# Exponentials read back in one piece, two rows sent through DRAM, the last norm on ScalarE, and a new table of due times

## The chip, the cores and the metric

The kernel runs on one core of a Trainium2 chip. A core has a matrix engine (TensorE, PE; its weight loads are listed as PEld), a vector engine (VectorE, DVE), an engine for activation functions (ScalarE, ACT), a general engine (GpSimd, POOL) and a queue engine (SyncE, SP). Each runs its own list of instructions in order and waits on semaphores for the others. SBUF and PSUM are the on-chip memories, DRAM the memory off the core's engines; 16 DMA engines move data between SBUF and DRAM, and in this kernel SP issues all of the transfers. The metric is the device time of one execution in microseconds (us), taken as a median.

## The reference

There are 64 independent graphs of 256 nodes with 256 features, each with a dense 256 x 256 matrix `adj`. Four layers follow each other, each wrapped as `x = layernorm(x + layer(x, adj))`; all is float32.

```python
# layer 0, 4 heads
att = sigmoid(q @ k.T * scale);  adj_h = adj * att
dis = where(deg > 0, deg ** -0.5, 0)         # deg: row sums of adj_h
Y = (dis[:, None] * adj_h * dis[None, :]) @ X;  layernorm of Y
# layer 1, 8 heads
out = softmax(where(adj > 0, q @ k.T / sqrt(32), -9e15)) @ v;  out @ Wo
# layer 2
h = ((adj @ x) + eps * x) @ W1                # 256 -> 1024
h = silu(h * rsqrt(mean(h ** 2) + 1e-6) * w);  h @ W2
# layer 3
Wh = x @ W;  e = leaky_relu(s1[:, None] + s2[None, :], 0.2)   # s = Wh @ a
h = softmax(where(adj > 0, e, -9e15)) @ Wh;  gelu(layernorm(h))
```

After layer 3 comes the last residual layernorm, and its result is written out.

## The kernel before, in words

**Tiles.** A graph's 256 x 256 matrix is one SBUF tile of 128 partitions x 512: two blocks of 128 rows side by side. A PSUM tile of 128 x 512 holds one result; there are eight. A matmul with a full 128 x 128 weight block and 256 columns takes 379 ns in the profile, and a product of two 256 x 256 matrices is eight of them. Heads are packed: products over 32 or 64 rows (L610, L517) or columns (L654, L557) of the array run beside each other, and the array changes its tiling between such groups and full ones.

**Recording.** The function `graph` records the operations of one graph, and `weights` those that load the constants. An `Op` has its engine, a cost, what it reads and writes, and a due time. Nothing is emitted yet. `Plan.order` then gives every operation the time `TIMES[stage][i] + PERIOD * graph + shift`, where `SHIFTS` holds a correction for the first ten and the last ten graphs, moves it behind what it depends on, and sorts all operations of all 64 graphs by it. Each engine runs its operations in that order. So the table decides how some sixteen graphs overlap: from the sixteenth graph on, the order of every engine is one ring that repeats for each graph, with layer 3 of graph g beside layer 2 of g+3, layer 1 of g+6 and layer 0 of g+9 to g+15. While it walks through the sorted list, `Plan.order` keeps a clock for each engine from the costs, the transfers' sizes and `AFTER`, and from it takes which of the freed buffers a new value gets (`SLOTS`: 46 tiles of kind `s`, 8 PSUM tiles, and so on). The order alone is fixed; when an instruction really starts is up to the semaphores.

**Transposes through DRAM.** For most graphs a transpose is done without PE. DVE transposes blocks of 32 x 32 into `eb`, SP writes `eb` to a DRAM tile `far`, and SP reads it back in another arrangement: `far_transposed` (L341 and L345 for layer 3's `x3` and exponentials, L349 and L351 for layer 0's result) and `far_shuffled` (L365, L368) for layer 1's input. Layer 1's exponentials of four heads (1 MB) are written in one piece (L638) and read back by four DMAs of 256 KB, one for each 32 partitions (L640). The 16 reciprocals of layer 1's softmax go the same way: `rT` is written (L662), and eight DMAs spread each head's row over 32 partitions as `rb` (L664). SP must wait for a write to land before it issues the reads, and everything behind it in SP's order waits too. The first graph or two, and the last three, use PE for some transposes (`NEAR`), because there PE has room.

**1/rms in layer 2.** The squares are summed over features by DVE (L712, L714) and PE (L719), DVE transposes the sums (L724), and POOL takes the power -1/2 (L727, L728), with one value for each token on its partition. PE then transposes this column, broadcast over 128 columns, into a PSUM tile `pr` (L734): a row of all tokens' factors on every partition. DVE multiplies `hT` by it, four of its eight feature blocks at a time (L738), ACT applies SiLU to the same four (L740), and the second product (L748) starts with the first four blocks of the first 128 tokens.

**Source terms in layer 3.** The product with `W` (L766) has two more columns, s1 and s2. ACT copies it to SBUF as `v3` (L770). PE transposes the column s2 in the same way as above into a PSUM tile (L775), and ACT adds s1 and s2 and applies the leaky relu (L779). The masked softmax follows (L479 on DVE, L484 on ACT), then the transpose through DRAM, then the product with `v3` (L395, shown as `ps<-v,eT`).

**The last norm.** `normed` scales a tile by its mean and 1/std. It does so on ACT (L433, after a small DVE step L429 that makes the bias), except for the final output `o`, which DVE scales (L437), but for the last three graphs. The statistics before it are DVE (L408) and POOL (L418, L419).

Of the kernel before, what the change touches and what calls it, by code (L numbers as in the profile page):

```python
# [10 lines left out]
AF = mybir.ActivationFunctionType  # L11
# [10 lines left out]
ITSELF = {"PE": 0, "DVE": 95, "ACT": 110, "POOL": 60, "SP": 0}  # L22
# [7 lines left out]
WORDS = {"s": 516, "d": 1024, "D": 2048, "b": 2048, "c": 32, "p": 512, "h": 2048, "t": 64, "f": 64}  # L30
# [4 lines left out]
SLOTS = {"s": 46, "d": 4, "D": 3, "b": 3, "c": 48, "p": 8, "h": 8, "t": 4, "f": 8}  # L35
DRAM = "hf"

PERIOD = 43736
TIMES = {
    "layer 0": [  # L40
        -319197, -113134, -100311, -71943, -247582, -546773, -546197, -131479, -172183, -152737, -281181, -565681,
        -397076, -73203, -63226, -95801, -374920, -232479, -110173, -195319, -301144, -87568, -115747, -89221,
        -90086, -83471, -69397, -574845, -68313, -63683, -428221, -63434, -57858],
    "y0": [
        -87831, -373130, -729274, -232310, -329503, -339824, -34600, -122314],
    "norms 0": [
        -317272, -27512, -143897, -30800, -393826, -114681, -25085, -20328, -60191, -14285, -14265],
    "x1": [
        -22878, -260036, -13056, -13194, -13556, -13246],
    "heads": [  # L50
        21083, -12704, 13821, -24706, 13005, -13170, 13837, -243391, -83618, -466639, 65818, -265435, 73110, 19862,
        -107166, -118808, 21980, 10121, -275945, 21957, 26901, 32166, 11340, -329066, -182994, -323173, -75745,
        23608, -95248, -264825, 13387, -31944, -232536, 41219, 50698, 41160, 52922, 28312, -12692, -142068, -83953,
        -450779, 19466, -393926, -133764, -346231, -789118, -242927, -827390, -284889, -296678, -73296, -150845,
        -367335, -429493, 32181, -382155, -84424, 31380, -400219, -232968],
    "layer 1": [
        -292171, -332905, -463540, -325283, -585287, 54654, -66521, -251318, -276322, -295456, -30216, 56307,
        -65386, -78434, 90307, -434932, 90241, 94160, -199479, 105185, -121163, 74219],
    "layer 2": [
        66102, 101580, 177708, 111997, -117369, -27941, 133669, -117923, -217828, -152742, -387796, 14051, 133564,  # L60
        -41433, -84629, -56243, 16618, 145648, 143272, 133937, 24587, 13427, -80823, 118404, -142608, -160852,
        137148, 118595, 74825, 145580, -289804, 60052, -166924, -3431, 150662, -168456, 169799, 100755, -8045,
        -471077, -194813, 118328, 190096, 218554, -9065, -135959, 207336, 166957, 235618, 218069, 181347, 233128],
    "x3": [
        242366, 185230, -3212, -59473, -20723, -54583, -119866, 144254, 154213],
    "layer 3": [
        276836, 259792, 276501, -11693, 283684, -160488, 83664, 237473, 286462, 287575, 288330, 294217, 114279,
        319058],
    "e3": [
        225632, 186632, 248234, -95896, 188509, 303747, 315177, 308934, 314526],  # L70
    "y3": [
        333821, 231651, 225040, 337186, 347307, 141236, 74504, 323745, 319142, 172218],
    "out": [
        334941, 353102, 351242, 369427, 456102, 453662, 446905],
    "weights": [
        -333952, -983130, -30359, -945696, -210686, -73894, -223709, -154959, -259880, -310601, -338541, -184949,
        -17446, 19612, -13322, 128972, -450356, 155594, -891871, -209532, -91470, -340360, 222543, -16205, -130618,
        97522, 87637, 248749, 277347],
    "y0 by PE": [
        -120210, -72674, -129154],  # L80
    "x1 by PE": [
        40623, 22839, -152651],
    "heads by PE": [
        -95458, 77404, 47061, -40228, 43109, -4907, 56735, -22684, 19941, -35811, 65682, 81329, -109895, -10708,
        -24959, 38549, 42640, 69976, 56753, -178021, -23198, -13718, 28668, 75592, -98145, 73422, 31198, 55531,
        51235, 24844, 60763, -27793, -9752, -23467, 70477, 25989, 2382, 78742, 63564, 1293, -164472, 35182, -52610,
        -16683, 12602, 7517, 71887, -71844, 77285, 75027, 82487, 60185, -10300, 9378, -10435, 69079, -8590, -59124,
        -58302, 76358, -3250, 77148, -45408],
    "x3 by PE": [
        269122, 230913],  # L90
    "e3 by PE": [
        314157, 165939],
    "y3 at the end": [
        325747, 321623, 301166, 221044, 338410, 229419, 304128, 177370, 248843, 349261, 270321],
    "out at the end": [
        364545, 252476, 378560, 444095, 457987, 508323, 479204, 533265],
}
SHIFTS = {
    0: (49484, -2460, -1572, -677, -2727),
    1: (4489, -16790, -1941, 1285, -26679),  # L100
    2: (-452, 1099, -750, -3702, 2374),
    3: (2324, -1473, -1339, -733, -695),
    4: (-50857, -1286, 113, -692, -3911),
    5: (-742, -320, -1324, 277, 36812),
    6: (103, 289, -690, -555, 30699),
    7: (-196, 1000, 88, -352, 20200),
    8: (651, 1253, -472, -442, 34933),
# [116 lines left out]
def two(v):  # L224

    return v.t.rearrange("p (n c) -> p n c", n=2)
# [662 lines left out]
```

## Time and profile before

| what | value |
|---|---|
| median of 3 runs | 2807.56 us (2806.32 to 2807.71) |
| the profiled execution | 2815.73 us |
| its span, first to last instruction | 2813.9 us |
| PE busy | 2652.4 us, 94% |
| DVE busy | 2441.4 us, 87% |
| ACT busy | 2192.5 us, 78% |
| POOL busy | 603.8 us, 21% |
| mean granted PE clock | 0.986 |
| DMA packets of the kernel's queue | 751776, 530.93 MB, 74.5% of 16 engines |

How to read it: busy time is the time in which an engine runs an instruction; registers, branches, semaphores and the issue of DMAs don't count. A group line names the source line, the engine, the operation, `out<-in` by the program's names, the shapes and the count; after the first bar stand the group's busy time in us and the mean of one in ns, after the second the time that the engine sat idle before them, and what ended most of it. A line of waits gives who waited for whom, the total in us, how often, and the longest. SPq is SP's list of DMA issues. A name such as `eT` is used for several tiles: the exponentials of layer 1 (four reads of 256 KB) and of layer 3 (four reads of 64 KB). Matmul records of one group appear as twice the program's matmuls.

### The profile page before, as it was taken

The numbers are of one execution on the slowest core, as the hardware profiler recorded it, in microseconds if no ns is written. First come the engines' busy times: TensorE is split into PE (matmuls) and PEld (weight loads), VectorE is DVE, ScalarE is ACT, GpSimd is POOL, SyncE is SP. The second block draws the span as 40 slices with busy tenths as digits, with TensorE's granted clock in tenths as the row PEclk, the third lists the DMA queues.
The fourth block names the chain that finished last, engine by engine and source line by source line (L and its number), as shares of the span: only waits on it lengthen the run. The fifth ranks groups of instructions, "written<-read, shape, count | busy, mean of one in ns | idle before, by whom it ended". The sixth has DMA issues, their size and how long they took to land.

```text
span 2813.9 us, 54722 instructions
## 1 busy us (share of the span) xinstructions
PE 2652.4 (94%) x17252; PEld 2143.6 (76%) x17252; DVE 2441.4 (87%) x6391; ACT 2192.5 (78%) x5278; POOL 603.8 (21%) x966
## 2 busy tenths in 40 slices
PE   7999999999999999999999999999999999999986
PEld 6778778887887787777877877778778778877765
DVE  4788889998999898898988988889889889989866
ACT  2778778788887887778877878788778777887776
POOL 1111212222222221212212222122122121222222
PEclk9999999999999999999999999999999999999998
DMA  4378878877878877878878778788787787787762
GB/s 135 91 206 211 204 183 202 208 211 188 215 208 198 212 197 179 210 199 189 204 185 202 196 182 211 195 190 202 187 203 196 184 203 206 192 206 199 197 137 75
DMA packets 752066, 534.44 MB, mean 190 GB/s; under 512 B 507936, under 2 KB 606624, under 8 KB 735904
## 3 DMA queue, kind: packets, MB, share of 16 engines
q1 hardware_dynamic: 751776, 530.93, 74.5%
q8 instruction: 138, 2.26, 0.4%
q14 instruction: 152, 1.25, 0.2%
HBM read 317.86 MB, written 212.86 MB: 189 GB/s over the span
## 4 chain that ended last, share of the span: by engine, by line
PE 46%; DMA 25%; DVE 19%; SPq 5%; ACT 3%; issue 3%; DVEq 0%; POOLq 0%; ACTq 0%; POOL 0%
DMA eT<-far 14%; PE ps L700 8%; PE ps L384 8%; PE ps L748 8%; PE ps L395 8%; DVE e L479 4%; DVE eb L633 4%; DMA far<-rT 4%; SPq L664 3%; PE av L654 3%; PE ps L557 2%; PE ps L517 2%; DMA far<-eb 2%; PE ps L610 2%; PE ps L766 2%
## 5 line engine op out<-in xcount | busy, mean ns | idle before, releaser
L418 POOL TENSOR_SCALAR mv<-mv 128x2 f32<-128x2 f32 x384 | 109.5, 285 | 2085.2 <-DVE mv L414 752.0
L484 ACT ACTIVATE e<-e,r 128x256 f32<-128x256 f32 x1024 | 506.0, 496 | 18.1 <-DVE r L479 17.4
L748 PE MATMUL ps<-w,hT 128*128 128x256 f32 x2048 | 462.9, 379 | 0.0
L700 PE MATMUL ps<-aggT,w 128*128 128x256 f32 x2048 | 461.9, 379 | 0.0
L700 PEld LDWEIGHTS ps<-aggT,w 128*128 128x128 f32 x2048 | 389.1, 190 | 52.9
L748 PEld LDWEIGHTS ps<-w,hT 128*128 128x128 f32 x2048 | 387.6, 190 | 52.0
L479 DVE CUSTOM_DVE_ANT_0 e<-ps,adj 128x256 f32<-128x256 f32 x1024 | 367.0, 419 | 25.0 <-PE ps L610 16.0
L419 POOL TENSOR_TENSOR mv<-mv,mhalf 128x2 f32<-128x2 f32 x384 | 331.2, 863 | 32.1
L707 ACT ACTIVATE hT<-ps,br,r 128x256 f32<-128x256 f32 x512 | 315.4, 625 | 0.0
L433 ACT ACTIVATE x<-y,mv 128x256 f32<-128x256 f32 x384 | 204.5, 595 | 131.7 <-PE ps L395 74.5
L633 DVE STREAM_TRANSPOSE eb<-e 128x1024 f32<-128x1024 f32 x248 | 289.1, 1204 | 0.0
L705 ACT ACTIVATE sq<-ps,b 128x256 f32<-128x256 f32 x512 | 241.9, 510 | 6.2 <-PE ps L700 6.2
L408 DVE BATCH_NORM_STATS2 mv<-y 128x6 f32<-128x512 f32 x320 | 222.3, 695 | 6.6
L395 PE MATMUL ps<-v,eT 128*128 128x256 f32 x512 | 141.9, 426 | 84.6 <-DMA eT<-far 41.9
L740 ACT ACT_TABLE_LOAD x63 | 80.8, 1283 | 167.4 <-DVE hT L738 167.1
L395 PEld LDWEIGHTS ps<-v,eT 128*128 128x128 f32 x512 | 102.7, 209 | 117.8 <-issue 31.0
L484 ACT ACTIVATION_READ_ACCUMULATOR e<-e,r 128x1 f32 x1024 | 192.3, 188 | 0.0
L523 DVE TENSOR_TENSOR att<-att,adjT 128x512 f32<-128x512 f32 x256 | 166.1, 674 | 14.1 <-ACT att L521 14.1
L740 ACT ACTIVATE hT<-hT 128x1024 f32<-128x1024 f32 x128 | 130.0, 1051 | 40.3 <-DVE hT L738 38.6
L654 PE MATMUL av<-eT,v 128*32 128x256 f32 x2048 | 126.7, 388 | 31.2 <-ACT x L433 20.8
L505 DVE TENSOR_TENSOR v<-ps,b_l 128x512 f32<-128x512 f32 x64 | 44.1, 690 | 127.2 <-PE ps L610 76.9
L610 PE MATMUL ps<-kT,qT 32*128 32x256 f32 x2048 | 152.0, 409 | 1.1 <-ACT kT L596 1.1
(121 smaller groups left out, 5538.8 us busy)
## 6 DMA issues: line engine op xcount, KB each, us to landing
far<-eb SPq DMA_DIRECT2D x124, 1024.0 KB, 5.6
eT<-far SPq DMA_DIRECT2D x496, 256.0 KB, 6.6
far<-eb SPq DMA_DIRECT2D x126, 256.0 KB, 2.8
xT<-far SPq DMA_DIRECT2D x496, 64.0 KB, 2.3
far<-eb SPq DMA_DIRECT2D x488, 64.0 KB, 2.8
x0T<-in_xT SPq DMA_DIRECT2D x64, 256.0 KB, 3.1
adjT<-in_adjT SPq DMA_DIRECT2D x64, 256.0 KB, 4.9
x<-in_x SPq DMA_DIRECT2D x64, 256.0 KB, 3.2
```

The lines of the kernel that those rows point to most:

```text
L384: pe.matmul(two(ps)[:, o, :], w.t[:, k, o * P:(o + 1) * P], way(two(xT)[:, k, :]), start=(k == 0), stop=(k == DB - 1))
L395: pe.matmul(two(ps)[:, n, :], two(xT)[:, k, n * P:(n + 1) * P], w()[:, k, :], start=(k == 0), stop=(k == DB - 1))
L408: op("DVE", 612, lambda: dve.bn_stats(mv.t[:, :6], src.t.rearrange("p (n c) -> p c n", n=NB)), [mv], [src])
L419: pool.tensor_tensor(m()[:, :, 0], m()[:, :, 0], c.mhalf[:, :NB], OP.pow)
L479: op("DVE", 345, lambda n=n: dve.tensor_tensor_reduce(out=E(n), in0=two(logits)[:, n, :], in1=two(negmask)[:, n, :], scale=-scale, scalar= ...
L484: op("ACT", 491, lambda n=n: act.activation(E(n), E(n), AF.Exp, bias=L(n), scale=-1.0, accum_out=r.t[:, col(n):col(n) + 1]), [(e, part(n)) ...
L633: op("DVE", 1155, lambda e=e, eb=eb, pair=pair: dve.transpose(eb.t.rearrange("p (b t g i) -> p t g b i", b=4, t=2, i=32)[:, pair], e.t.rea ...
L654: pe.matmul(two(av)[i * HD1:(i + 1) * HD1, hq, :], two(v1)[:, m, h * HD1:(h + 1) * HD1], eTs[h // 2][1](i % 2, m), start=(m == 0), stop=(m ...
L700: pe.matmul(two(ps)[:, i, :], c.w2_1.t[:, k, (j + i) * P:(j + i + 1) * P], two(aggT)[:, k, :], start=(k == 0), stop=(k == DB - 1))
L705: op("ACT", 357, lambda ps=ps, sq=sq, i=i, j=j: act.activation(two(sq)[:, i, :], two(ps)[:, i, :], AF.Square, bias=c.b2_1.t[:, j + i:j + i ...
L707: op("ACT", 452, lambda ps=ps, i=i, j=j: act.activation(Hb(j + i)[:, 0], two(ps)[:, i, :], AF.Identity, bias=c.br2.t[:, j + i:j + i + 1], ...
L748: pe.matmul(two(ps)[:, n, :], Hb(j)[:, 0, n * P:(n + 1) * P], c.w2_2.t[:, j, :], start=(j == 0), stop=(j == HB - 1))
```

## The change

- Layer 1's exponentials are written to DRAM in four pieces of 256 KB, rearranged on the way, and read back whole by one DMA of 1 MB. There are as many DMAs as before.
- For the first 61 graphs the row of 1/rms and the row of source terms no longer come from PE. A new helper `over_partitions` takes a small tile that DVE has transposed, writes it to DRAM, and reads a row from it onto all partitions by four DMAs. That is one DVE transpose and five DMAs for each of the two rows. The row lies in SBUF (kind `w`, four tiles) with its 32-token blocks in another order, which the reading instructions undo by their access patterns. The last three graphs keep the transposes on PE.
- `hT` is multiplied and passed through SiLU by halves of the tokens (all eight feature blocks of 128 tokens), not by halves of the feature blocks, and the second product needs only the half of its own tokens.
- The final norm is scaled by ACT for all graphs.
- `PERIOD`, `TIMES` and `SHIFTS` are new throughout, with stages for the new parts. So is the order of every engine, and with it the choice of buffers. Costs and sizes by which the planner's clock runs are changed (they shape the choice of buffers), there are 43 instead of 46 tiles of kind `s`, 8 instead of 4 of kind `t`, and 12 instead of 8 small DRAM tiles.

The diff, without the numbers of the tables:

```diff
-ITSELF = {"PE": 0, "DVE": 95, "ACT": 110, "POOL": 60, "SP": 0}
+ITSELF = {"PE": 0, "DVE": 130, "ACT": 110, "POOL": 60, "SP": 0}
...
-SLOTS = {"s": 46, "d": 4, "D": 3, "b": 3, "c": 48, "p": 8, "h": 8, "t": 4, "f": 8}
+SLOTS = {"s": 43, "w": 4, "d": 4, "D": 3, "b": 3, "c": 48, "p": 8, "h": 8, "t": 8, "f": 12}
...
-PERIOD = 43736
+PERIOD = 49305
...
+    def over_partitions(src, at):
+        far, dst = Value("f", "far"), Value("w", "row", 4)
+        op("SP", 500, lambda: nc.sync.dma_start(far.t, src.t), [far], [src], after=2600, size=36)
+        for q in range(4):
+            op("SP", 500, lambda q=q: nc.sync.dma_start(
+                dst.t[32 * q:32 * q + 32].rearrange("p (a m) -> p a m", a=4),
+                far.t.rearrange("(a c) m -> c a m", a=4)[at][None].to_broadcast([32, 4, 64])), [(dst, q)], [far], after=1900, size=37)
+        return dst
...
     def normed(src, name):
-        if name != 'o' or b >= plan.graphs - ENDS:
-            op("DVE", 70, lambda: dve.scalar_tensor_tensor(
-                m()[:, :, 1], m()[:, :, 1], -1.0, m()[:, :, 0], op0=OP.mult, op1=OP.mult), [mv], [mv])
+        op("DVE", 70, lambda: dve.scalar_tensor_tensor(
+            m()[:, :, 1], m()[:, :, 1], -1.0, m()[:, :, 0], op0=OP.mult, op1=OP.mult), [mv], [mv])
...
-            op("DVE", 328, lambda n=n: dve.tensor_scalar(
-                two(dst)[:, n, :], two(src)[:, n, :], m()[:, n, 1:2], m()[:, n, 0:1],
-                op0=OP.subtract, op1=OP.mult), [(dst, n)], [(src, n), mv])
+            op("ACT", 492, lambda n=n: act.activation(
+                two(dst)[:, n, :], two(src)[:, n, :], AF.Identity, bias=m()[:, n, 1:2], scale=m()[:, n, 0:1]),
+                [(dst, n)], [(src, n), mv])
...
-            eb, far, eT = Value("D", "eb", 2), Value("h", "far"), Value("D", "eT", 4)
+            eb, far, eT = Value("D", "eb", 2), Value("h", "far", 4), Value("D", "eT")
...
-        op("SP", 500, lambda eb=eb, far=far: nc.sync.dma_start(far.t, eb.t), [far], [eb], after=5500, size=700)
         for q in range(4):
-            op("SP", 500, lambda far=far, eT=eT, q=q: nc.sync.dma_start(
-                eT.t[32 * q:32 * q + 32].rearrange("j (a g) -> j a g", a=4),
-                far.t.rearrange("(a j) (b g) -> b j a g", a=4, b=4)[q]), [(eT, q)], [far], after=5000, size=178)
+            op("SP", 500, lambda eb=eb, far=far, q=q: nc.sync.dma_start(
+                far.t.rearrange("(b j) (a g) -> a j b g", a=4, b=4)[q],
+                eb.t[32 * q:32 * q + 32].rearrange("j (b g) -> j b g", b=4)), [(far, q)], [eb], after=2000, size=180)
+        op("SP", 500, lambda far=far, eT=eT: nc.sync.dma_start(eT.t, far.t), [eT], [far], after=2400, size=850)
...
-    hT = Value("b", "hT", HB)
+    hT = Value("b", "hT", NB * HB)
...
+    last = " by PE" if b >= plan.graphs - NEAR[2] else ""
+    if last:
+        ...
+        op("PE", 2 * PE_TR, fn, [pr], [rs], mode="transpose")
+    else:
+        back, by = Value("t", "back"), "p (a n i) -> p n a i"
+        op("DVE", 163, lambda: dve.transpose(back.t, rs.t), [back], [rs])
+        pr = over_partitions(back, 0)
-    for j in range(0, HB, 4):
-        four = [(hT, i) for i in range(j, j + 4)]
-        op("DVE", 1130, lambda j=j: dve.tensor_tensor(
-            Hb(j, 4), Hb(j, 4), pr.t[:, None, :N].to_broadcast([P, 4, N]), OP.mult), four, [*four, pr])
-        op("ACT", 965, lambda j=j: act.activation(Hb(j, 4), Hb(j, 4), AF.Silu), four, four, table=SILU)
+    for n in range(NB):
+        half = [(hT, NB * j + n) for j in range(HB)]
+        mine = lambda n=n: Hb(0, HB)[:, :, n * P:(n + 1) * P]
+        op("DVE", 1130, lambda n=n, mine=mine: dve.tensor_tensor(
+            mine().rearrange("p j (a i) -> p j a i", a=4), mine().rearrange("p j (a i) -> p j a i", a=4),
+            pr.t[:, :N].rearrange(by, n=NB, a=4)[:, n][:, None].to_broadcast([P, HB, 4, 32]), OP.mult), half, [*half, pr])
+        op("ACT", 965, lambda mine=mine: act.activation(mine(), mine(), AF.Silu), half, half, table=SILU)
...
-            op("PE", 4 * PE_MM, fn, [(ps, n)], [c.w2_2] + [(hT, j) for j in js] + [(ps, n)] * half)
+            op("PE", 4 * PE_MM, fn, [(ps, n)], [c.w2_2] + [(hT, NB * j + n) for j in js] + [(ps, n)] * half)
...
+    if last:
+        ...
+        op("PE", 2 * PE_TR, fn, [s2], [v3], mode="transpose")
+    else:
+        turned, by3 = Value("t", "turned"), "p (a n i) -> p n a i"
+        op("DVE", 163, lambda: dve.transpose(turned.t.rearrange("p (n k) -> p n k", n=NB), V3()[:, :, D - 30:]), [turned], [v3])
+        s2 = over_partitions(turned, 31)
...
-        op("ACT", 360, lambda n=n: act.activation(two(e)[:, n, :], s2.t[:, :N], AF.Prelu, bias=s1(n), alpha=0.2),
+        op("ACT", 400, lambda n=n: act.activation(
+            two(e)[:, n, :].rearrange("p (n a i) -> p n a i", n=NB, a=4), s2.t[:, :N].rearrange(by3, n=NB, a=4), AF.Prelu, bias=s1(n), alpha=0.2),
```

In the new order, a graph's ring on SP holds 62 DMAs (52 before). On PE the two layer 1 score groups (L610) of a graph follow the product `ps<-v,eT` at once and three groups later; before, the first stood half a ring ahead of the second.

## The prediction

> **What bounds the kernel now.** I read the busy shares first, then the stretches, the waits of TensorE (PE), and then the waits and the timeline of the queue that they lead to.
>
> ```profile
> PE 2652.4 (94%) x17252; PEld 2143.6 (76%) x17252; DVE 2441.4 (87%) x6391; ACT 2192.5 (78%) x5278; POOL 603.8 (21%) x966
> ```
>
> PE is the busy engine; its idle 161 us are what a new order can win. The stretches (span, busy time of PE, PEld, DVE, ACT, POOL, granted clock, DMA share, GB/s) show that they are not there from the start:
>
> ```profile
> 620.00:920.00 300.00, 296.17 (x1935) 242.02 (x1934) 281.46 (x723) 247.49 (x588) 69.10 (x107) 1.00 0.80 209
> 1200.00:1500.00 300.00, 283.89 (x1852) 230.94 (x1848) 265.49 (x695) 236.56 (x571) 65.08 (x105) 1.00 0.79 196
> ```
>
> From 620 to 920 us PE is 99% busy, later 95%. The timeline of PE shows one ring of each kind, from the last matmul group of one graph (`ps<-v,eT`) on:
>
> ```profile
> 607.69 1.97 PE L395 MATMUL ps<-v,eT 128*128 128x256 f32 x8 [0.69 <-DVE low L479]
> ...
> 648.10 1.89 PE L395 MATMUL ps<-v,eT 128*128 128x256 f32 x8
> ...
> 1281.08 1.97 PE L395 MATMUL ps<-v,eT 128*128 128x256 f32 x8 [1.62 <-DMA eT<-far]
> 1282.98 1.15 PE L610 MATMUL ps<-kT,qT 32*128 32x256 f32 x16
> 1284.98 1.93 PE L654 MATMUL av<-eT,v 128*32 128x256 f32 x32 [0.86 <-ACT x L433]
> ```
>
> 648.10 - 607.69 = 40.4 us a graph is PE's own work; from about the nineteenth graph on the starts of this group lie 42.5 us apart. What comes too late is `eT`, layer 3's transposed exponentials, read back through DRAM. The waits, first PE's, then those of SP, the queue that issues every DMA (total us, times, longest):
>
> ```profile
> PE ps L395 <- DMA eT<-far: 41.9, 24, 3.0
> PE av L654 <- ACT x L433: 20.8, 25, 1.1
> ...
> SPq L664 <- DMA far<-rT: 165.4, 64, 4.1
> SPq L351 <- DMA far<-eb: 164.7, 63, 5.2
> SPq L345 <- DMA far<-eb: 112.1, 68, 3.8
> SPq L345 <- DMA eT<-far: 65.0, 100, 1.1
> ```
>
> SP issues in order and stands still for a write to DRAM before it may read it back; everything behind it is late. One such place in SP's timeline:
>
> ```profile
> 1344.42 0.39 SPq L662 DMA_DIRECT2D far<-rT  x1
> 1344.90 1.04 SPq L638 DMA_DIRECT2D far<-eb  x1
> 1348.42 3.14 SPq L664 DMA_DIRECT2D rb<-far  x6
> 1351.61 2.80 SPq L640 DMA_DIRECT2D eT<-far  x6
> 1354.51 1.20 SPq L345 DMA_DIRECT2D eT<-far  x2
> ```
>
> One DMA stands between the write of `rT` and its reads, so SP waits 2.4 us; then six reads of 256 KB go out ahead of layer 3's, which need 8.0 us to land (median). From 500 to 2500 us the trace gives, per graph of 42.5 us: 52 DMAs with 26.9 us in issue (0.52 each), 2.5 us of steps between them, 1.8 us in semaphore instructions and 11.3 us of other waiting, of which some 2.6 us is for VectorE (DVE) and the rest for transfers. SP sets the pace, with no slack of its own.
>
> **What the Trainium skill says.** "DMA: Bandwidth & Descriptors", section Anatomy of one DMA, gives a DMA a fixed cost of about 2 us, most of it the receipt of the last byte; 64 KB reads here land in 2.1 us, 16 KB of `rT` in 4.0. Its Rules for kernel authors ask that a DMA which reads what another wrote waits for the first one's semaphore: that is SP's wait above. "TensorE: Matmul & The Clock Gate", section HAM oscillation, says an idle window of about 3.4 us halves PE's clock: the trace agrees, eleven spells of 3.4 or 6.8 us at half clock lie between 390 and 2720 us, mostly beside the longest waits; 51 us in all, 25 us lost. "Perfetto Trace Analysis", section Optimizing Scalar/DVE Operations, gives DVE 60 ns access on SBUF and 125 on PSUM, ScalarE (ACT) 93 and 51; here 128x512 additions take 680 ns from SBUF, 683 from PSUM, so the trace shows no such gap for DVE.
>
> **The change part by part,** per graph, 61 of 64 graphs.
>
> PE: two pairs of transposes go.
>
> ```profile
> L734 PE MATMUL pr<-ident,rs 128*128 128x128 f32 x128 | 27.5, 297 | 0.0
> L775 PE MATMUL s<-ident,v 128*128 128x128 f32 x128 | 27.5, 296 | 1.2 <-ACT v L770 1.2
> ```
>
> 55 us of busy time, but not 55 us of gain: they stood behind row-tiled matmuls, and changing tiling costs time anyway. From the fourth last L610 matmul to the third of the full group behind it: 1.03 us with a pair between, 0.86 us without; for L517 1.23 to 1.40 against 1.06. The new order also changes tiling more often. Summed by the starts of groups in the trace: before, 15 full groups of eight at 1.726, L766 1.744, the two behind transposes 1.623 and 1.622, and rows, columns and transposes 1.081 + 1.859 + 1.877 + 1.931 + 0.466 + 0.681 + 0.165 + 0.921 + 0.464: 40.32 us. After: 14 x 1.726 + 1.744, full groups behind L610, L517 and L535 at 1.919, 1.920 and 1.818, and 1.081 + 1.872 + 1.864 + 0.165 + 0.921 + 1.931 + 0.681: 40.08 us. That is -0.24 x 61 = -15 us.
>
> DVE: the last norm leaves it (2 x 0.402), its bias step (0.153) and two small transposes (0.24 each, as L724) come: -0.2 us on some 38.3. The multiplication of `hT` stays 2 x 1.21 by the SBUF/PSUM comparison above; bounds -0.1 (the skill's PSUM price) to +1.0 us (strided halves; unshown). DVE has 1.8 us of cover below 40.1; beyond that each us costs 61. ACT: +2 x 0.595 us, on 34: hidden in its 5 us of idle; without that cover +60 us. The additions of source terms read SBUF instead of PSUM: within 0.1 us. Table loads stay 3.9 a graph by the order. POOL's work is unchanged.
>
> DMA time: a packet of 2 KB takes 155 ns where the exponentials are being read, 102 where they are not, 85 to 94 as a write; 8 KB written takes 320. Exponentials before: 2 x 8 x 0.320 + 64 x 0.155 = 15.0 us on each of 16 engines. After: 64 x 0.085 to 0.102 as writes, and 2 x 8 packets of 8 KB read, between 0.320 and 0.620 (the 2 KB price by bytes): 10.5 to 16.4. I take 0.40: 12.5. The rows add ten DMAs of 128 packets of 256 B (18 ns): 1.5 us. In sum -1 us on 33 (-3 to +3).
>
> SP: 62 DMAs instead of 52. At 0.48 us for an undisturbed issue with its step that is 29.8 us; at today's mean of 0.57, 35.3. What it saves is waiting. By the new order eleven DMAs stand between `rT`'s write and the first `rb` read (before: one), fourteen between the 1/rms rows' write and read, seven for the sources, three for `yT` (before: none), thirteen for layer 3's `xT` (before: none). Of 2.6 + 2.6 + 1.8 us a graph (165.4, 164.7 and 112.1 us over 64) about 1.5 stays. Every DMA also waits for the one eight before it (seen as L345 waiting for `eT<-far`); a whole 1 MB read, by the 1 MB write's 5.6 us, holds the eighth DMA behind it 2 to 3 us. Queued behind SP's waits are then `rb`, the sources' write, `x3`'s write and the loads. 29.8 + 1.2 (slower strided issues) + 1.5 + 3 + 2 (waits for DVE) = 37.5 us, below PE's 40.1.
>
> Chain to layer 3's `eT`: the new detour adds a transpose (0.24), a write (2.7 to 4) and a read (2.3) to it, and the PE work between L766's group and the reading group falls from some 51 to 45 us by the same group times. Summing durations along the new order I get the rows landing 9 us into the ring, where ACT has idle time until the aggregate at 13; layer 3's exponentials leave DVE at 21, their write SP at 27, the reads at 31, landing at 37, needed at 40. So 3 us of slack, and what would be late next is the sources' row. First `rb`, 1/rms and exponentials have 3 to 5 us.
>
> PE's waits: L395's idle is 84.6 us, L654's 31.2. Of the 95 us that PE idles between 400 us and the drain and the 25 us of slow clock I take two thirds: -80. With -15 for PE, -4 for an earlier first matmul (its load now stands behind five DMAs instead of eight, one of them 1 MB), nothing for the drain, whose last three graphs keep the transposes: -99. Span 2813.9 - 99 = 2715, with 1.8 around it 2717; the median lies 8 below the profiled execution (2807.56 to 2815.73): 2709, say 2710 us.
>
> **The rivals.** (a) Partial: the new ring settles at 41.5 to 42 instead of 40.5, since DVE's cover is 1.8 us, or whole reads cost 0.62: 2745 to 2795 us. For it: DVE is 94% busy in the best stretch. (b) The wait only moves: the sources' row or the whole read takes `eT`'s place and the ring stays at 42.5: 2795 less PE's 15 and some noise, 2790 to 2813. For it: the order is rigid, and a single late transfer held the ring before. (c) Slower: SP is the bound. At 0.57 an issue, 35.3 us, waits above 4.8 us a graph cost PE its floor, above 7.2 the kernel is slower than now. If the 8.7 us of transfer waits of today survive, the ring is 44 us: 1.5 x 61 = +92, 2900; with 1 us less 2840. For it: ten more DMAs on the busiest queue, and single large reads. Against it: the places named above. (d) The rewritten exponential transfers do nothing, since 2 KB packets merely move to the write side: against it the 85 to 94 ns; then (a) holds.
>
> **How the numbers follow.** A measurement of this kernel tells 0.2%, 6 us. Chances: forecast (2665 to 2745) 0.52, (a) with (d) 0.20, (b) 0.07, (c) 0.21. Of (b) about half is within 0.2%. Faster 0.75, same 0.04, slower 0.21. The forecast's low end is every wait gone, 2807 - 95 - 25 - 15 = 2672; 2660 takes in cheaper reads. 2660 to 2850 leaves out little below and the worse half of (c).
>
> **What would show it.** Right: starts of the `ps<-v,eT` group 40 to 41 us apart to the end, L395's idle under 30 us, SP waits for `rT` and `yT` under 1 us a graph, DMA share not above 0.85, `eT` whole landing in 5 to 7 us. Wrong: SP without a gap and PE waiting for `rb`, `hT` or `eT`; ACT waiting for the sources' row at the Prelu over 2 us a graph; the `hT` multiplication over 1.5 us. The prediction falls if the ring is above 42.5 us.

## The result, and the profile after

| | before | after |
|---|---|---|
| median | 2807.64 us (2806.32 to 2813.96) | 3191.78 us (3183.65 to 3197.86) |
| ratio, 95% interval | | 1.1361 (1.1326 to 1.1396) |
| span of the profiled execution | 2813.9 us | 3196.1 us |

The change made the kernel 13.6% slower; 2710 us was predicted. The busy shares and the kernel's DMA queue, from the page of the kernel after:

```profile
PE 2769.7 (87%) x17008; PEld 2194.5 (69%) x17008; DVE 2427.4 (76%) x6452; ACT 2252.4 (70%) x5397; POOL 635.4 (20%) x966
...
q1 hardware_dynamic: 839616, 550.96, 62.3%
```

Of the 382 us more, 117 are PE's busy time, the rest its idle time. The share of DMA time fell (74.5% before): the packets took 1991 us on each engine instead of 2096, in a span that is 382 us longer. So the DMA engines are not short of time; they stand still in between. The same two stretches as before (span, busy time of PE, PEld, DVE, ACT, POOL, granted clock, DMA share, GB/s), and one of 6 us:

```profile
620.00:920.00 300.00, 264.42 (x1622) 210.13 (x1619) 235.10 (x618) 211.87 (x519) 61.38 (x92) 0.95 0.65 177
1200.00:1500.00 300.00, 262.01 (x1622) 208.82 (x1620) 233.75 (x621) 218.49 (x530) 60.84 (x92) 0.94 0.66 180
...
1609.00:1615.00 6.00, 3.43 (x16) 2.65 (x14) 0.00 (x0) 0.00 (x0) 0.00 (x0) 0.97 0.08 22
```

No good stretch is left, and in the third the DMA engines are 8% busy, at 22 GB/s, while DVE and ACT do nothing. SP's timeline (start, length, what is issued) shows what was in the queue then (L390 is the read of a row):

```profile
1607.45 1.88 SPq L390 DMA_DIRECT2D row<-far  x4
1609.38 0.43 SPq L352 DMA_DIRECT2D far<-eb  x1
1609.91 0.38 SPq L326 DMA_DIRECT2D adj<-in_adjS  x1
1610.33 0.45 SPq L658 DMA_DIRECT2D eT<-far  x1
1610.87 0.52 SPq L356 DMA_DIRECT2D eT<-far  x1
1611.49 2.15 SPq L680 DMA_DIRECT2D rb<-far  x1
```

The four reads of the 1/rms row land 3.9, 4.9, 6.7 and 7.6 us after their issue, the last at 1616.6. Transfers of 256 KB and of 1 MB stand in the queue behind them, and yet from 1608.5 to 1614.5 only some 71 packets of 256 B start per us. DVE waits 9.3 us for the row, and PE's matmuls behind DVE (`deg`) are late in turn; the timelines of DVE, and of PE one graph earlier:

```profile
1616.67 1.23 DVE L763 TENSOR_TENSOR hT<-hT,row 128x1024 f32<-128x1024 f32 x1 [9.34 <-DMA row<-far]
...
1524.42 1.89 PE L417 MATMUL ps<-v,eT 128*128 128x256 f32 x8
1568.96 3.78 PE L406 MATMUL ps<-xT,w_q 128*128 128x256 f32 x8 [6.85 <-DVE deg L555]
1574.82 1.89 PE L417 MATMUL ps<-v,eT 128*128 128x256 f32 x8
```

The `ps<-v,eT` groups lie 50.4 us apart here, 48.8 on average from 500 to 2500 us. The eight matmuls behind the gap take 3.78 us instead of 1.89: half clock. The Trainium skill ("TensorE: Matmul & The Clock Gate", HAM oscillation) says that an idle window of about 3.4 us halves it. In this trace each of the 51 gaps of PE that are longer is followed by half clock, but so are 14 of the 34 gaps of 1 to 3.4 us. The span holds 67 spells of half clock with 457 us in all, against 16 with 79 us before. The waits (total, times, longest):

```profile
DVE hT L763 <- DMA row<-far: 467.1, 60, 10.9
PE ps L406 <- DVE deg L555: 172.3, 33, 7.7
...
ACT e L811 <- DMA row<-far: 113.8, 23, 10.7
...
SPq L362 <- DMA far<-eb: 191.7, 49, 6.9
SPq L680 <- DMA eT<-far: 89.4, 58, 3.0
```

SP's wait for `rT` is all but gone, as forecast (7.4 us in all, 165.4 before). That for layer 0's transpose (L362) is not: its write stands behind the reads of the source terms' row and lands after 6.3 us (median from 500 to 2500 us) instead of 3.0.

### The profile page after: what moved, and what is told of

The parts are those of the page before. It is cut to its first block, busy times and chain, and to the rows that moved or that the text cites. A ratio compares the mean times of both kernels' runs of the same rounds, so it can differ in the third digit from the quotient of the medians.

```text
span 3196.1 us, 55053 instructions
## 1 busy us (share of the span) xinstructions
PE 2769.7 (87%) x17008; PEld 2194.5 (69%) x17008; DVE 2427.4 (76%) x6452; ACT 2252.4 (70%) x5397; POOL 635.4 (20%) x966
## 3 DMA queue, kind: packets, MB, share of 16 engines
q1 hardware_dynamic: 839616, 550.96, 62.3%
## 5 line engine op out<-in xcount | busy, mean ns | idle before, releaser
L440 POOL TENSOR_SCALAR mv<-mv 128x2 f32<-128x2 f32 x384 | 133.1, 347 | 1919.5 <-DVE mv L430 1448.9
L763 DVE TENSOR_TENSOR hT<-hT,row 128x1024 f32<-128x1024 f32 x122 | 148.8, 1219 | 478.5 <-DMA row<-far 467.1
L716 PE MATMUL ps<-aggT,w 128*128 128x256 f32 x2048 | 473.7, 384 | 16.2 <-ACT aggT L397 8.7
L406 PE MATMUL ps<-xT,w_q 128*128 128x256 f32 x512 | 178.7, 510 | 174.6 <-DVE deg L555 172.3
L453 ACT ACTIVATE x<-y,mv 128x256 f32<-128x256 f32 x384 | 216.8, 597 | 157.0 <-DVE mv L450 149.3
L649 DVE STREAM_TRANSPOSE eb<-e 128x1024 f32<-128x1024 f32 x248 | 300.8, 1230 | 11.1 <-ACT e L500 9.2
L723 ACT ACTIVATE hT<-ps,br,r 128x256 f32<-128x256 f32 x512 | 297.0, 580 | 0.0
L406 PEld LDWEIGHTS ps<-xT,w_q 128*128 128x128 f32 x512 | 127.7, 257 | 212.9 <-DVE deg L555 185.7
L811 ACT ACTIVATE e<-row,v 128x256 f32<-128x256 f32 x122 | 55.6, 500 | 264.1 <-DMA row<-far 113.8
L559 POOL TENSOR_TENSOR dp<-dp,mhalf 128x8 f32<-128x8 f32 x64 | 120.8, 1888 | 509.9 <-DVE dp L558 440.9
```

The source lines that it names most:

```text
L406: pe.matmul(two(ps)[:, o, :], w.t[:, k, o * P:(o + 1) * P], way(two(xT)[:, k, :]), start=(k == 0), stop=(k == DB - 1))
L453: op("ACT", 492, lambda n=n: act.activation(two(dst)[:, n, :], two(src)[:, n, :], AF.Identity, bias=m()[:, n, 1:2], scale=m()[:, n, 0:1]), ...
L649: op("DVE", 1155, lambda e=e, eb=eb, pair=pair: dve.transpose(eb.t.rearrange("p (b t g i) -> p t g b i", b=4, t=2, i=32)[:, pair], e.t.rea ...
L716: pe.matmul(two(ps)[:, i, :], c.w2_1.t[:, k, (j + i) * P:(j + i + 1) * P], two(aggT)[:, k, :], start=(k == 0), stop=(k == DB - 1))
L723: op("ACT", 452, lambda ps=ps, i=i, j=j: act.activation(Hb(j + i)[:, 0], two(ps)[:, i, :], AF.Identity, bias=c.br2.t[:, j + i:j + i + 1], ...
```

## The experiments

Theory 1: the reads of a row stall the DMA queue. Theory 2: 62 DMAs a graph are too many for SP. Theory 3: the reads stand too late in SP's order. The kernel before took 2808 us in the comparison above and 2814 to 2818 in those below, so kernels are set against each other by their ratios to it.

**Another copy for each partition.** `root` is the one column of `rs` with the 1/rms; the source terms' transpose takes its column in the same way.

```diff
-dve.transpose(back.t, rs.t)
+dve.transpose(back.t.rearrange("p (n k) -> p n k", n=NB), root()[:, :, None].to_broadcast([P, NB, 32]))
 ...
-far.t.rearrange("(a c) m -> c a m", a=4)[at][None].to_broadcast([32, 4, 64])
+far.t.rearrange("(a r) m -> r a m", a=4)
```

> Edit: the two transposes ahead of the rows take their one column 32 times over, so that all 32 rows of each block of 32 in DRAM hold the row, and partition p reads the copy of its own instead of all 32 partitions reading one. Same count of instructions and DMAs, same bytes, same packets of 256 B, same order. Theory 1 (the four reads of a row fetch the same four DRAM pieces of 256 B 128 times each, these fetches are served one after another, some 48 ns each by the trace, and the queue stands still for 6 us behind them): the reads land in 2 to 3 us instead of 5.2, VectorE's wait for the row at L763 falls from 467 us to under 60, ring 42 to 44 us, 2700 to 2850 us. Theory 2 (62 DMAs a graph are too many for SP): 3150 to 3230, as the changed kernel. Theory 3 (the reads of 1/rms stand too late in SP's order, behind eight writes of exponentials): also within 60 us of the changed kernel, as the order is the same.

2825.08 us, ratio 1.0034 (1.0022 to 1.0046). The DMA view (KB each, median us to landing) and the waits of this kernel:

```profile
row<-far SPq DMA_DIRECT2D x488, 32.0 KB, 2.4
...
DVE hT L764 <- DMA row<-far: 196.7, 58, 7.8
```

Nearly the whole loss is gone, with the same instructions, DMAs, bytes and order: theory 1. From the first issue to the last landing a row takes 4.6 us (median) instead of 9.2. But the kernel is not faster than before, and DVE still waits more than expected.

**Rows by PE.** Both rows come from PE's transposes for every graph, as before the change.

```diff
-    if last:      # roots, sources: last three graphs
+    if True:
```

> Edit: both rows made by PE's transposes for every graph, as in the kernel before; all else (whole read of the exponentials, halves of the hidden layer, norm on ACT, table) as in the changed kernel; 52 DMAs a graph instead of 62. All theories expect most of the loss back: 2700 to 2850. By theory 1 it comes within 60 us of the kernel with spread copies; by theory 2 it is at least 200 us faster than that; by theory 3 likewise. If it stays above 3000, the rows are not what costs, and the new order is.

2767.61 us, ratio 0.9822 (0.9800 to 0.9844): 2% below the copies. Something else about the rows through DRAM costs that.

**Reads earlier.** The four reads of 1/rms are to stand ahead of the exponentials' writes in SP's order.

```diff
 "roots": [
-    159480, -143449, 166730, 178540, 167878, 166683],
+    159480, -143449, 163300, 163300, 163300, 163300],
```

> Edit: the four reads of 1/rms stand ahead of the eight writes of exponentials in SP's order instead of behind them, some 6 to 8 us earlier; still 128 fetches of each piece. Theory 3: VectorE's wait at L763 falls from 467 us to under 150, and the time to 2800 to 2950. Theory 1: the queue stands still just as long, only at another place, now ahead of the exponentials' writes: the reads still land in 5 us or more, the share of DMA time stays near 62%, 3050 to 3250. Theory 2: as the changed kernel, 3150 to 3230.

3594.11 us, ratio 1.276 (1.2723 to 1.2798). The edit had done more than was meant: an operation stands behind all that it depends on, and without the due time 178540 DVE's first multiplication of `hT` moved some ten instructions forward, to where the row had not landed. DVE waited 799.7 us there. The run doesn't test theory 3; with the multiplication's due time kept it was run again:

```diff
+"layer 2 on": [178541, ...     # was 161859; DVE's order as in the changed kernel
```

> Edit: the reads of 1/rms ahead of the exponentials' writes again, 128 fetches of each piece as in the changed kernel, and the first multiplication kept at its place in VectorE's order (due time 178541), which the first such run had moved along with the reads. Theory 3 (the reads stand too late): VectorE's wait for the row at L763 falls from 467 us to under 100 and the time to 2800 to 2950. Theory 1 (place): the reads land no faster (median about 5 us), what stands behind them on the queue is late, now the writes of exponentials; 3000 to 3250.

3100.22 us, ratio 1.1000 (1.0972 to 1.1028). DVE's wait for the row is all but gone (4.3 us in all), and about a quarter of the loss with it (1.1361 to 1.1000), but not the rest. The DMA view and SP's waits of this kernel:

```profile
row<-far SPq DMA_DIRECT2D x488, 32.0 KB, 5.2
far<-eb SPq DMA_DIRECT2D x622, 256.0 KB, 5.7
...
SPq L362 <- DMA far<-eb: 198.7, 49, 6.4
```

The reads land no sooner, and now the exponentials' writes behind them take 5.7 us (4.2 in the changed kernel). Most of the wait was moved, not removed: the reads' place in the order has a part, but theory 3 does not explain the loss; theory 1 stands.

**What stalls: the single DMAs.** Theory 1 had put it to each piece of 256 B being fetched 128 times. A kernel that leaves out all computation issues such reads alone, in sets of four DMAs with 512 packets in all (128 in the set with the row as 1 KB). The four-piece set, and the set with a piece for each partition:

```diff
+nc.sync.dma_start(row[32 * q:32 * q + 32]..., far.rearrange("(a c) m -> c a m", a=4)[0][None].to_broadcast([32, 4, 64]))
+nc.sync.dma_start(row[32 * q:32 * q + 32]..., far.rearrange("(a r) m -> r a m", a=4))
```

> Only DMAs on an empty machine (all computation left out): sets of four reads, each of 32 partitions by four packets of 256 B, that fetch from 1, 4, 8, 16 or 128 different pieces of 256 B in DRAM (each set twice), and from 4 neighbouring pieces; then one set with a load of 256 KB behind it, once with 4 pieces and once with 128. From the first issue of a set to its last landing, theory 1: 1 piece about 25 us, 4 pieces 7 to 9 us, 8 pieces 4 to 5, 16 pieces 3 to 4, 128 pieces 2.5 to 4 (the issues of four DMAs alone take 1.5 to 2); the load behind 4 pieces lands 3 us or more later than the one behind 128. Theories 2 and 3: all sets alike within 1 us, as the packets are of one size and count.

From first issue to last landing (second sets): 1 piece 7.4 us, 4 pieces 4.3, 8 pieces 5.3, 16 pieces 4.2, 128 pieces 3.2, the 1 KB 3.4. The last set of 4 pieces, alike but for its buffer in DRAM, took 7.6. So a rate for each piece is wrong: one piece takes no longer than the four of that buffer, and the four of the other take little more than half as long. The load meant to follow the stalled set was issued elsewhere and tells nothing. This led to two theories. A: a place in DRAM (pieces at some addresses share one) has the rate, whichever of its pieces are wanted. B: each piece has a rate of its own. Four pieces `s` times 256 B apart, by one DMA:

```diff
+nc.sync.dma_start(row..., piece[0:4 * s].rearrange("(a c) m -> c a m", a=4)[0][None].to_broadcast([P, 4, 64]))
```

> Only DMAs, one at a time, each over 128 partitions, all computation left out: a row as one packet of 1 KB (128 fetches); then 512 fetches of 256 B from one piece (at two addresses), and from four pieces 512 B, 1, 2, 4, 8, 16 and 32 KB apart, and 8 KB apart at another start. Theory A (places of some rate, 84 fetches a us each, as the sets of four reads showed it: one piece 6 to 7 us, four pieces of one buffer 4.4 us, four pieces of another 7.6 us): one piece takes 6 us over the 1.7 of any small transfer at either address; four pieces take the same 6 us at the distances where they share a place, 3 us where they fall on two places, 1.5 on four; the row of 1 KB 1.5 us over it. Theory B (sameness of the piece): four pieces always take a quarter of one piece, 1.5 us.

The sets overlapped, since each had its own buffer. Landings followed the ones before by 6.3 and 3.6 us (one piece, two addresses), 0.5 to 0.6 (four pieces, 512 B to 2 KB apart), 3.0 (4 KB), 7.0 (8 KB), 5.3 (16 KB), 3.1 (32 KB), 4.8 (8 KB, other start): theory A, but not clean. In turn, with one buffer for all, and without the small write to DRAM behind each set:

```diff
-row = sb.tile([P, 256], F32, name=name)      # in every set
+row = sb.tile([P, 256], F32, name="row")     # once
```

> Only DMAs, each issued when the one before has landed (in the run before they ran into each other), all computation left out: a row as one packet of 1 KB; 512 fetches of 256 B from one piece (at two addresses); from four pieces 512 B, 1, 2, 4, 8, 16 and 32 KB apart; four more with 8 KB at other starts; and a load of 256 KB issued right behind a read with 8 KB, with 512 B and with one packet of 1 KB. Theory A: one piece 7.5 to 8.5 us from issue to landing; 512 B to 2 KB 2.5 to 4; 4 and 32 KB about 5; 8 KB between 5 and 8.5 by its start; the load behind 8 KB lands 3 us or more later than the one behind 512 B. Theory B: all sets of four pieces alike.

| 128 partitions fetch | us to landing | packets a us |
|---|---|---|
| 1 KB as one packet (128) | 2.8 | 82 |
| one piece of 256 B (512), two addresses | 7.7, 7.7 | 81, 81 |
| four pieces (512), 512 B, 1, 2 KB apart | 3.0, 3.1, 3.2 | 316, 308, 322 |
| 4 KB, 16 KB, 32 KB apart | 4.4, 7.0, 4.4 | 169, 91, 169 |
| 8 KB apart, five starts | 7.7, 4.4, 7.7, 7.2, 7.6 | 81, 170, 81, 91, 81 |

But for the two of 91, the rates are some 81 times one, two and four. So theory A says that a place serves some 81 fetches a us (12 ns each), of one piece or of several that share it; 128 fetches of the same 1 KB go at that rate too. The 512 B set is not at the engines' limit: in the trace of before, 569 packets of 256 B start in the fullest 0.5 us. A load of 256 KB issued behind the 8 KB set landed after 8.1 us, behind the 512 B set after 3.5. Three stretches of this kernel, within the first one-piece read, the 512 B set and the 4 KB set (span, busy time of DVE and POOL, granted clock, DMA share, GB/s), show how a stalled queue looks idle:

```profile
11.50:19.00 7.50, 0.00 (x0) 0.00 (x0) 1.00 0.07 17
28.00:31.00 3.00, 0.07 (x1) 0.00 (x0) 1.00 0.19 44
39.00:43.50 4.50, 0.21 (x1) 0.00 (x0) 1.00 0.12 29
```

**In the kernel: four pieces at two distances.** In both runs, only the four pieces of a row are written.

```diff
-    far.t.rearrange("(a c) m -> c a m", a=4)[at][None].to_broadcast([32, 4, 64])
+    far.t[:8].rearrange("(a z) m -> z a m", a=4)[0][None].to_broadcast([32, 4, 64])    # 512 B
+    far.t.rearrange("(a c) m -> c a m", a=4)[0][None].to_broadcast([32, 4, 64])        # 8 KB
```

> Edit: of each row only its four pieces are written, 512 B apart, and the four reads fetch them as in the changed kernel: 512 packets of 256 B from four pieces, each fetched 128 times, 62 DMAs, same order. Theory A (places): pieces 512 B apart lie in different places or in one that is not slowed (they cost no visible time among the single DMAs), so the reads land in 2 to 3 us and the time is that of the copies, 2800 to 2850. Theory B (each piece is served at its own rate, whatever its place): 128 fetches a piece as before, 3150 to 3230.

> Edit: the same, with the four pieces 8 KB apart as in the changed kernel (only the write is smaller: 4 packets instead of 128). Both theories: as the changed kernel, 3150 to 3230; if it falls below 3100, the size of the write had a part in it.

512 B: 2827.16 us, ratio 1.0050 (1.0036 to 1.0064). 8 KB: 3195.44 us, 1.1357 (1.1340 to 1.1375). DVE's wait for the row, first 512 B, then 8 KB:

```profile
DVE hT L764 <- DMA row<-far: 202.1, 58, 8.0
```

```profile
DVE hT L764 <- DMA row<-far: 470.9, 61, 11.6
```

Each piece is fetched 128 times in both. Where the pieces lie is worth 13%, and the size of the write nothing. That the addresses decide, with the same fetches of each piece, is shown; why addresses 8 KB apart fall together is not.

**What is left of the rows: DMAs on SP.** The row's pieces side by side, a partition's row one packet of 1 KB:

```diff
-    nc.sync.dma_start(far.t, src.t)
+    nc.sync.dma_start(far.t[:4], src.t.rearrange("(a c) m -> c a m", a=4)[at])
 ...
-    far.t.rearrange("(a c) m -> c a m", a=4)[at][None].to_broadcast([32, 4, 64])
+    far.t[:4][None].to_broadcast([32, 4, 64])
```

> Edit: of each row only its four pieces are written to DRAM, side by side, so that a partition reads its row as one packet of 1 KB: the same 62 DMAs a graph in the same order, but 128 fetches a row instead of 512 (and 4 packets written instead of 128). Theory A (fetches from one place of DRAM go at some 84 a us, whether they want one piece or four; what matters is their number and how many places they hit): the reads land in about 2 us, as with the copies, and the stall is gone though all 128 fetches hit the same 1 KB. What is left over the kernel with rows by PE (58 us between 2825 and 2768) is then SP's load of ten DMAs more: 2790 to 2830. Theory B (it is the sameness of the address): the reads land in 4 us or more and the time is over 2900.

2818.69 us, ratio 1.0011 (1.0002 to 1.0021). The four reads of a row then made one:

```diff
-    for q in range(4): nc.sync.dma_start(dst.t[32 * q:32 * q + 32]..., far.t[:4][None].to_broadcast([32, 4, 64]))
+    nc.sync.dma_start(dst.t.rearrange("p (a m) -> p a m", a=4), far.t[:4][None].to_broadcast([P, 4, 64]))
```

> Edit: as the row of 1 KB, and the four reads of a row made one DMA over 128 partitions: 56 DMAs a graph instead of 62. If SP's load is what is left: 2745 to 2785, within 20 us of rows by PE (52 DMAs). If it is not SP but the rows' way through DRAM (a chain of write, read and wait that is longer than PE's transpose), it stays at the time of the kernel with four reads, within 10 us.

3097.21 us, ratio 1.0996 (1.0980 to 1.1013): the same slip as with the earlier reads; again the multiplication had moved and DVE waited 481.5 us. With its due time kept:

```diff
+"layer 2 on": [178541, ...     # was 161859
```

> Edit: the row of 1 KB in one read (56 DMAs) again, but with the due time of the hidden layer's first multiplication put to 178541. In the run before, taking away the read with the latest due time (178540) had let that multiplication move some ten instructions forward in VectorE's order, ahead of the masks of layer 0, so that it waited for the row there; that run compared two orders, not two numbers of DMAs. Now VectorE's order is that of the changed kernel. If SP's load is what is left over the kernel with rows by PE: 2755 to 2800. If not: 2810 to 2830, as with four reads.

2765.25 us, ratio 0.9820 (0.9796 to 0.9843). Six DMAs fewer a graph are worth 1.9% (the last part of a row is also issued sooner; the two are not told apart). From 500 to 2500 us a graph took on SP:

| us a graph | copies (62 DMAs) | one read (56) | rows by PE, below (52) |
|---|---|---|---|
| issue | 35.3 | 33.3 | 30.2 |
| steps and semaphores | 4.1 | 3.5 | 3.3 |
| waits | 3.2 | 4.9 | 8.6 |
| sum | 42.6 | 41.7 | 42.1 |

With 62 DMAs SP, at 0.57 us an issue, waits for only 3.2 of 42.6 us. The Trainium skill ("DMA: Bandwidth & Descriptors", Rules for kernel authors) advises one transfer over 128 partitions instead of several over parts; here that is worth the 1.9%.

The same due time on top of rows by PE:

```diff
+"layer 2 on": [178541, ...     # was 161859
```

> Edit: rows by PE, with the first multiplication at the place in VectorE's order that it has in the changed kernel (in the run with rows by PE it stood some ten instructions earlier, as PE's row has an earlier due time). If the 58 us between spread copies and rows by PE come from that place: 2800 to 2830. If they come from SP's ten DMAs and the rows' way through DRAM: 2760 to 2780.

2763.53 us, ratio 0.9805 (0.9788 to 0.9823): the multiplication's place is not what sets rows by PE and the copies apart. Without the stall and with one read, the rows through DRAM are as fast as rows by PE (0.9820 against 0.9805 and 0.9822), not faster.

**The other parts.** Norm back on DVE, and the exponentials' transfers as before, both on top of rows by PE; then all parts of the change undone but the table.

```diff
+    if name == 'o' and b < plan.graphs - ENDS: op("DVE", 328, ... tensor_scalar ...)
```

> Edit: the kernel with rows by PE, with the last norm of inner graphs back on VectorE (2 operations of 328 ns instead of one of 70 ns and two of 492 ns on ScalarE). By the prediction's sum (VectorE at 87%, work before its operations hidden) it does nothing: 2760 to 2775. If VectorE's order sets the ring, +0.6 us a graph: 2795 to 2810.

```diff
-    four writes of 256 KB, op("SP", 500, ... dma_start(eT.t, far.t) ...)
+    op("SP", 500, ... dma_start(far.t, eb.t) ...), four reads of 256 KB
```

> Edit: the kernel with rows by PE, with the exponentials' transfers as before the change (one write of 1 MB in packets of 8 KB, four reads in packets of 2 KB, at the place of the whole read). If the whole read is what the prediction took it for (eT lands earlier, DMA engines less crowded): 2790 to 2830, the DMA share up from 72% to 75%, PE's wait for eT at L417 from under 20 us to over 60. If the gain over the kernel before comes from the order and the halves alone: 2760 to 2780.

```diff
-    for n in range(NB): halves of the tokens, hT in NB * HB parts
+    for j in range(0, HB, 4): halves of the features, hT in HB parts
+    (with the two edits above)
```

> Edit: every operation as in the kernel before (rows by PE, exponentials by one write and four reads, the hidden layer in quarters by hidden feature, last norm on VectorE), with only the changed kernel's table of due times and slots. If the gain of the kernels with rows by PE over the kernel before (40 us) is the new order's: 2760 to 2785. If it is that of the halves of the hidden layer, which let the first product of W2 start after half the tokens: 2790 to 2815.

2772.59 us (0.9847, 0.9833 to 0.9862), 2769.45 us (0.9835, 0.9820 to 0.9849) and 2774.00 us (0.9844, 0.9826 to 0.9863), against 0.9822 with all parts but the rows. The new order alone, with its numbers of buffers, gives 1.6%; with rows by PE, norm and whole read are not told from nothing, nor is there room for much from the halves. The DMA queue with the whole read, then with four reads:

```profile
q1 hardware_dynamic: 751776, 530.93, 72.0%
```

```profile
q1 hardware_dynamic: 751776, 530.93, 76.1%
```

The whole read does take 1.9 us a graph off each DMA engine (4.1% of 2768 us, over 61), and no time follows.

**Both ways.** One read of 1 KB, with rows by PE in the last 11 graphs.

```diff
-    last = " by PE" if b >= plan.graphs - NEAR[2] else ""
+    last = " by PE" if b >= plan.graphs - 11 else ""      # x3 and e3 keep NEAR[2]
```

> Edit: the kernel with the row of 1 KB in one read (56 DMAs, VectorE's order kept), with both rows by PE in the last 11 graphs, where PE stood still for 27 us behind late transfers. If the rows' way through DRAM costs nothing in the middle and 27 us at the end: 2740 to 2757, faster than either. If the end's waits have another source: 2760 to 2770.

2753.57 us, ratio 0.9773 (0.9759 to 0.9787): faster than the kernel before and the changed one. Its busy shares:

```profile
PE 2647.3 (96%) x17040; PEld 2119.3 (77%) x17040; DVE 2410.9 (88%) x6436; ACT 2252.7 (82%) x5397; POOL 638.5 (23%) x966
```

## Why the prediction was wrong, step by step

- **"The rows add ten DMAs of 128 packets of 256 B (18 ns): 1.5 us", and "a read (2.3)".** This step failed. It priced a row's packets by the time that a packet is recorded with, and that time (15 ns) is not what a packet costs when all want one place. At 81 a us, 512 packets take 6.3 us, with the 16 engines 8% busy; in the changed kernel a row took 9.2 us from first issue to last landing, and held up what stood behind it. Two rows a graph are, by the 6.3, 12.6 us of nearly standing queue, where the sum had 1.5 us of the engines' time. Of it 6.2 us a graph reached the end (48.8 against 42.6, from 500 to 2500 us), some 380 us over 61 graphs. By ratios, the stall is 1.1361 less 1.0034. The trace of before showed no read like it: the nearest, `rb`, goes through 32 pieces, each fetched 32 times, and in the changed kernel's trace its packets start at some 640 a us (1623.75 to 1624.50 us). The step gave no upper bound for that unknown. The fixed 2 us that the prediction quotes are stated in the Trainium skill ("DMA: Bandwidth & Descriptors", Anatomy of one DMA) for DMAs that GpSimd issues; here SP issues them, and a row read alone as packets of 1 KB landed after 2.8 us.
- **"First `rb`, 1/rms and exponentials have 3 to 5 us."** The wait came there: DVE waited 7.7 us a graph for 1/rms (467.1 over 61). The sources' row, named as next to be late, cost ACT 1.9.
- **SP "37.5 us, below PE's 40.1".** Wrong, and second in size. With the stall mended (the copies) an issue with its step took 0.62 us, not 0.48: 38.7 us a graph, and 42.6 with semaphores and waits. Rival (c) named SP as the bound, but its sum was too low as well: it took 35.3 us for issues and steps and put the point from which the kernel is slower than now at 7.2 us of waits; the copies had only 3.9 and came out 0.3% slower. The rival had the sign of the result, but not the stall, and its 2840 to 2900 was too low.
- **"SP waits for `rT` and `yT` under 1 us a graph."** Right for `rT`. For `yT` 3.1 us, because its write stood behind a stalled row.
- **What bounds the kernel before, and a new order as its cure.** Right in direction: the order alone gives 1.6%, some 44 us of the 80 expected of waits and clock, and PE's wait for `eT` falls from 41.9 to 7.0 us with it. But the ring fell from 42.6 to only 42.2 us (500 to 2500 us), not to 40.5, some 16 us in all; 18 us more are gained ahead of the first `ps<-v,eT` group, which starts at 297 us instead of 315. PE now waits for POOL, at the transpose of the 1/rms row: with rows by PE, rival (b), a wait that only moves, is right in part. PE's waits with the order alone:

```profile
PE pr L753 <- POOL rs L744: 61.9, 46, 2.7
...
PE ps L411 <- DMA eT<-far: 7.0, 3, 4.1
```

- **Exponentials: -2.5 us of DMA time a graph.** Measured -1.9; the size held, and no gain followed in the kernels with rows by PE, as in rival (d), although not for its reason: the DMA time did fall.
- **DVE and ACT.** The multiplication takes 1.219 us (1.21 predicted), the norm's move is hidden.
- **PE's -15 us.** Not seen: 2648.1 us busy with one read a row, 2643.6 with rows by PE (2652.4 before).
- **The clock.** Taken as a gain of part of 25 us; the gaps behind the stall turned it into a loss (457 us at half clock, 79 before). That the trace of before agrees with an idle window of 3.4 us was a misreading: the eleven spells last 3.4 or 6.8 us, but ten of them follow idle gaps of PE of only 2.0 to 3.3 us.

## What to carry to other kernels

Before a row is spread over partitions from DRAM, count how many fetches go to one place, not bytes or packets: keep the pieces side by side and fetch a partition's whole row as one packet, in one DMA over all partitions. Even so, compare it with a transpose on PE: here it was no faster until the last graphs went back to PE. When the share of DMA time falls while the kernel gets slower, look for a stretch in which the queue is full and the engines are idle, and for what stands at its head. When an order is sorted by due times, an edit to one operation moves what depends on it: compare the order of every engine before a run is read as a test of one thing.

## What was not expected of the hardware

- Where the fetched pieces lie in DRAM decides. 512 fetches of one piece of 256 B go at 81 a us, and so do those of four pieces 8 KB apart from three of five starts; at the other two they go at 91 and 170. Four pieces 512 B to 2 KB apart go at 308 to 322.
- Such fetches hold up other transfers of the queue: a load of 256 KB landed after 8.1 us behind them, instead of 3.5.
- The recorded time of the waiting packets does not grow (15 ns, against 17 at 316 a us), so a stalled queue looks idle: with the same packets and bytes, the share of DMA time is 62.3% in the changed kernel and 73.4% with a copy for each partition.
